# Four graph layers on one core: result scatters, shared queries, edge slots and weight parts moved in a hand-written order

## The chip, the cores and the metric

The kernel runs on one core of one Trainium2 chip. A core has five engines that run at the same time[...]: TensorE (PE, matmuls; its weight loads are listed as PEld), VectorE (DVE), ScalarE (ACT), GpSimd (POOL), and SyncE (SP), which here only issues DMAs. POOL issues DMAs too, those with indices (gathers and scatters). Each engine takes its instructions in the order in which the program lists them for it. The metric is the device time of one execution in microseconds. Before the change its median over three runs is 2139.91 us, from 2137.19 to 2143.26.

## The reference

A batch of 16 graphs shares one adjacency matrix of 1024 nodes in which an entry is set with probability 0.0078, so that a node has 8 neighbours on average. Node features have width 128. Layers 0, 2 and 3 are attention layers with 8 heads of 16 and a feed-forward part; layer 1 is a graph attention layer. Cut to what matters:

```python
def attention_layer(adj, h):                     # layers 0, 2, 3
    Q, K, V = h @ Wq, h @ Wk, h @ Wv             # per head: 8 heads of 16
    scores = where(adj == 0, -inf, Q @ K.T / 4)
    x = layer_norm(h + softmax(scores) @ V @ Wo + bo)
    return layer_norm(x + relu(x @ W1 + b1) @ W2 + b2)

def graph_layer(x, adj):                         # layer 1
    h = x @ W
    e = leaky_relu((h @ a_src)[:, None] + (h @ a_dst)[None, :], 0.2)
    return layer_norm(softmax(where(adj == 0, -inf, e)) @ h + x)

x = attention_layer(adj, x); x = graph_layer(x, adj)
x = attention_layer(adj, x); x = attention_layer(adj, x)
```

## The kernel before

The kernel uses the sparsity: it lists the neighbours of every node and touches only those (`sparse_path`). A second path for other matrices, `dense_path`, is skipped by a flag.

**Setup.** `graph` sorts the nodes by degree and finds, with VectorE's eight-largest instruction, the list of neighbours of each node. In the sorted order the nodes form 8 row blocks of 128. `slots` turns the lists of one block into gather indices (`idx`) and 0/1 matrices (`marks`): its inner function `spread` lays the lists out with small TensorE matmuls (L433, L441) into a PSUM bank; then VectorE reads that bank (L454 to L470). In the kernel before, the generator stops once after `spread`, then `WAIT` = 3 times more with the word "pass", then does the VectorE part. `load_weights` loads a layer's weights and prepares them: it centres Wo and W2 on VectorE (L485 to L487), multiplies W1 with b2 on TensorE (L524) and subtracts that from b1 on VectorE (L529). `load_graph_weights` does the like for layer 1: a transposition, a copy `wgT` (L551), a product with the two end vectors, a copy of it (L555), and a centring.

**Blocks.** The main loop runs over 64 units, here called blocks: 4 layers, 2 groups of 8 graphs, 8 row blocks. Blocks 0 to 7 are group 0 of layer 0, 8 to 15 its group 1, 16 to 31 layer 1, 32 to 47 layer 2, 48 to 63 layer 3. A block of an attention layer has five parts. A part handles two chunks; a chunk is one neighbour for each of 128 slots. The fourth part has a single chunk, the shared one, whose slots are taken from several neighbour columns. For every part:

- `gathered` issues on POOL one indirect DMA per chunk, the neighbours' keys and values (`e<-table,idx`, L968), four parts ahead, into one of four buffers; so it waits until VectorE has finished with the part that used the buffer.
- `products` multiplies keys and expanded queries on VectorE (L982). For the shared chunk POOL does this (L997, `product_of_shared`) two parts ahead, in place in the buffer `qx`, which SP filled before with pieces of the expanded queries (`shared`, DMA `qx<-qr`, L946). `qx` is single: it is free again when TensorE has summed the shared chunk of the block before.
- `exponentials` reduces the products on VectorE (L1015) and takes the exponential on ScalarE (L1019).
- `weighted`, one part later, multiplies values and exponentials on VectorE (L1043).
- `summed`, two parts later, adds the chunks with matmuls against `marks` into PSUM (L1059). When a block's last part is summed, `divided` sums the exponentials, takes reciprocals (L1096), divides (L1099) and starts two tails, one for each half of the group.

**Between the parts.** `others()` stands at three places of every part and hands out other work in small steps. From block 1's second part on a table (`PLANS`) tells which: "a" and "b" are a step of the tail of the first and second half; "q" is a step of `aside()`. A tail (`attention_tail`) does the output projection, the norms and the feed-forward part of the block before, on TensorE and ScalarE. Its end, `finish`, either transposes the new features and projects them for the next layer (stored on SP as `kept<-xT`, L575, and `table<-kv`, L592), or, in layer 3, transposes the result back, copies it on ScalarE (`outs`, L660) and issues on POOL the scatter of the result (L699, once per block; the very last block uses L693). `aside()` takes one step of the first generator in `fronts`; if that list is empty, of `loads` (the fetch of x for a block ahead, in layer 0 an indirect DMA and transpositions); and if both are empty, of `slow`, which in blocks 0 to 6 projects group 1 of layer 0 at leisure (`at_leisure`, L583 and L592). In the first two blocks one step of `slow` is handed out at every `others()` as well. What is left in `fronts` at the end of a block is done there at once.

**What stands in fronts.** For block 0: the five steps of the slots of block 1, the rest of the fetch of block 1 (`second`), the weight parts, the graph weight parts; in its second part the queries of block 1 are put behind all these. `queries` projects the queries on TensorE (L923), copies them (L927), repeats them over 128 partitions with matmuls (L932) and copies that (`qr`, L935). For each later block: in layer 0 the five steps of the slots of the next block, then the queries of the next block; in the fifth blocks of layers 1 and 2 (blocks 20 and 36) the weight parts of the next layer come before the queries.

In this order the instructions of all engines are written out; nothing is rearranged. Within a part, the order on POOL is: what `others()` brings (a scatter in layer 3), then `gathered`, then `product_of_shared`. `shared` comes in a block's second part, after `exponentials`:

```python
            others()
            if here:
                exponentials(i)
            if here and i == begun + 1:
                if is_attention(u):
                    shared(u)
```

Of the kernel before, what the change touches and what calls it, by code (L numbers as in the profile page):

```python
# [131 lines left out]
EDGES = 4  # L132
WAIT = 3
AHEAD = 4
# [11 lines left out]
def sparse_path(ctx: ExitStack, tc: tile.TileContext, a: dict, out: bass.AP, flag):  # L146
# [278 lines left out]
    def slots():  # L425
# [21 lines left out]
        for q in range(T):  # L447
            ps = spread(q)
            yield
            for _ in range(WAIT if q else 0):  # L450
                yield "pass"
            c, m = COLUMN[q, MIX, 0], MARK[q, 0, 0]
# [39 lines left out]
    def load_weights(layer):  # L492
# [35 lines left out]
        yield  # L528
        nc.vector.tensor_tensor(w[layer, "b1"], w[layer, "b1"], ps, ALU.subtract)  # L529
        nc.vector.tensor_tensor(w[layer, "ln1_b"], w[layer, "ln1_b"], w[layer, "b2"], ALU.add)  # L530
# [3 lines left out]
    def load_graph_weights():  # L534
# [15 lines left out]
        wgT = wts.tile([P, P], F32, tag="Wo", name="wgT")  # L550
        nc.vector.tensor_copy(wgT, ps)  # L551
        ps = bank([P, 2])
        nc.tensor.matmul(ps, wgT, ends, start=True, stop=True)
        yield
        nc.vector.tensor_copy(wg[:, D:], ps)  # L555
        centred(wg[:, :D], D)
# [109 lines left out]

    leaving = {}

    def finish(l, g, t, h, z, gain, shift, dve=False):
# [22 lines left out]
        if (l, g, t) == units[-1]:  # L692
            nc.gpsimd.indirect_dma_start(  # L693
                out=out.rearrange("n (k c) -> (n k) c", k=GR * HF),
                out_offset=bass.IndirectOffsetOnAxis(ap=halves[:, h : h + 1], axis=0),
                in_=o[:, h].rearrange("p g d -> p (g d)"), in_offset=None,
            )
        elif h + 1 == HF:
            nc.gpsimd.indirect_dma_start(  # L699
                out=out.rearrange("n (k c) -> (n k) c", k=GR),  # L700
                out_offset=bass.IndirectOffsetOnAxis(ap=places[:, g, t : t + 1], axis=0),
                in_=o.rearrange("p h g d -> p (h g d)"), in_offset=None,
            )

# [481 lines left out]
    with tc.manual_schedule():  # L1186
# [4 lines left out]
        next(entry)  # L1191
        more = [weights, load_graph_weights()]
        rest = slots()
# [31 lines left out]
        gathered(AHEAD - 1)  # L1225
        fronts.extend([islice(rest, WAIT + 2), second] + more)
        closing, sizes = None, ()
        begun = 0
        for i in range(len(parts) + 2):
            here = i < len(parts)  # L1230
            u = parts[i][0] if here else len(units)
            if here:
                l = units[u][0]
                eager[0] = 1 if u < 2 else 0
                if i and parts[i - 1][0] != u:
                    begun = i
                    if u < T - 1:
                        fronts.append(islice(rest, WAIT + 2))
                    if l + 1 < len(LAYERS) and LAYERS[l + 1][1] is ATTN:
                        if units[u][1:] == (0, 1):  # L1240
                            more = load_weights(LAYERS[l + 1][0])
                            next(more)
                            next(more)
                        if units[u][1:] == (0, 4):
                            fronts.append(more)
                if is_attention(u):
                    products(i)
            if i > 1:
                summed(i - 2)
                done = parts[i - 2][0]  # L1250
                if parts[i - 1 : i] == [] or parts[i - 1][0] != done:
                    closing = divided(done)
                    next(closing)
            others()
            if here:
                exponentials(i)
            if here and i == begun + 1:
                if is_attention(u):
                    shared(u)
                while loads:  # L1260
                    advance(loads)
                if u + 1 < len(units):
                    fronts.append(queries(u + 1))
                loads.append(loaded(u + 2))
# [3 lines left out]
            if 0 < i <= len(parts):  # L1268
# [4 lines left out]
                gathered(i - 1 + AHEAD)  # L1273
                product_of_shared(i + 2)
                for _ in sizes:
                    pass
# [27 lines left out]
        while opening[0] < len(plan[0]):  # L1304
            planned()
        while tails:
            advance(tails)
# [439 lines left out]
```

## Time and profile before

| what | value |
|---|---|
| median of 3 runs | 2139.91 us (2137.19 to 2143.26) |
| the profiled execution | 2128.25 us, span of its instructions 2126.4 us |
| first product of block 0 | 91.6 us |
| layer 0, blocks 0 to 7 and 8 to 15 | 306.4 and 269.5 us |
| layer 1 (16 blocks) | 316.5 us |
| layer 2 (16 blocks) | 536.7 us |
| layer 3 (16 blocks, with the end) | 605.7 us |
| mean granted TensorE clock | 0.973 |

The stretches in the table run from the first VectorE product of one block to that of another (L982; in layer 1 the first sum L1024). A line of a group of instructions in the profile reads: line of the kernel, engine, operation, output<-inputs with shapes, count, then busy time and mean duration in ns, then the idle time of the engine just before them and what ended it. A line of the chain of waits reads: who waited, for whom, us in total, times, the longest. Matmul counts are of the trace, in which each fp32 matmul can appear twice.

### The profile page before, as it was taken

The numbers are of one execution on the slowest core, as the hardware profiler recorded it, in microseconds if no ns is written. First come the engines' busy times: TensorE is split into PE (matmuls) and PEld (weight loads), VectorE is DVE, ScalarE is ACT, GpSimd is POOL, SyncE is SP. The second block draws the span as 40 slices with busy tenths as digits, with TensorE's granted clock in tenths as the row PEclk, the third lists the DMA queues.
The fourth block names the chain that finished last, engine by engine and source line by source line (L and its number), as shares of the span: only waits on it lengthen the run. The fifth ranks groups of instructions, "written<-read, shape, count | busy, mean of one in ns | idle before, by whom it ended". The sixth has DMA issues, their size and how long they took to land.

```text
span 2126.4 us, 37294 instructions
## 1 busy us (share of the span) xinstructions
PE 1955.3 (92%) x13444; PEld 1240.3 (58%) x13444; DVE 1818.9 (86%) x1320; ACT 1516.5 (71%) x5043; POOL 1173.0 (55%) x747
## 2 busy tenths in 40 slices
PE   7679999999999989998899999999999999999986
PEld 6455666656666555555465665666655555555544
DVE  6977889999997576677989999999998989988983
ACT  3447878888886555555587888888887787777764
POOL 3344555555556477684555555555555666656550
PEclk8789999999999999999999999999999999999998
DMA  7988888888998799998899999999998888788960
GB/s 271 347 283 287 316 295 297 305 298 305 316 314 297 234 338 355 320 365 310 311 321 323 329 339 314 331 336 337 332 314 274 301 277 306 249 298 279 296 223 22
DMA packets 164800, 636.10 MB, mean 299 GB/s; under 512 B 34664, under 2 KB 37480, under 8 KB 116110
## 3 DMA queue, kind: packets, MB, share of 16 engines
q0 software_dynamic: 88720, 485.08, 64.6%
q1 hardware_dynamic: 75888, 148.57, 21.6%
q8 instruction: 108, 1.77, 0.3%
q14 instruction: 84, 0.69, 0.1%
HBM read 581.08 MB, written 92.34 MB: 317 GB/s over the span
## 4 chain that ended last, share of the span: by engine, by line
PE 47%; DVE 17%; DMA 14%; issue 13%; POOL 5%; ACT 4%; POOLq 0%; DVEq 0%; ACTq 0%
DMA e<-table,idx 13%; PE acc L1059 12%; DVE pr L1043 5%; PE yps L752 5%; PE ps L738 5%; PE ps L654 5%; DVE pr L982 4%; POOL e L968 4%; PE ps L583 3%; PE ps L932 3%; DVE sc L1015 3%; PE yps L756 2%; PE yps L728 2%; PE yps L727 2%; PE ps L923 2%
## 5 line engine op out<-in xcount | busy, mean ns | idle before, releaser
L968 POOL DMA_INDIRECT e<-table,idx x576 | 890.2, 1545 | 683.9 <-DVE pr L1043 417.9
L1043 DVE TENSOR_TENSOR pr<-e,ex 128x2048 f32<-128x2048 f32 x272 | 630.0, 2325 | 76.7 <-ACT ex L1019 38.4
L1059 PE MATMUL acc<-pr,marks 128*32 128x512 f32 x2200 | 442.8, 621 | 57.5 <-DVE pr L1043 43.9
L982 DVE TENSOR_TENSOR pr<-e,qr 128x2048 f32<-128x2048 f32 x192 | 440.4, 2294 | 43.1 <-ACT qr L935 21.0
L1015 DVE TENSOR_REDUCE sc<-pr 128x128 f32<-128x2048 f32 x192 | 438.9, 2286 | 6.6
L631 ACT ACTIVATE z<-yps,root 128x128 f32<-128x128 f32 x888 | 314.3, 372 | 175.7 <-PE yps L756 124.6
L1059 PEld LDWEIGHTS acc<-pr,marks 128*32 128x32 f32 x2200 | 93.9, 111 | 292.6 <-issue 204.2
L752 PE MATMUL yps<-W,f 128*128 128x128 f32 x1520 | 249.8, 282 | 7.5 <-ACT f L747 5.6
L647 ACT ACTIVATE z<-yps,rstd 128x128 f32<-128x128 f32 x888 | 252.2, 369 | 3.5
L752 PEld LDWEIGHTS yps<-W,f 128*128 128x128 f32 x1520 | 203.5, 191 | 65.4 <-ACT f L747 29.0
L935 ACT COPY qr<-ps 128x512 f32<-128x512 f32 x384 | 204.0, 600 | 16.7 <-PE ps L932 15.8
L583 PE MATMUL ps<-Wkv,xT 128*128 128x256 f32 x768 | 199.7, 406 | 15.2 <-ACT xT L662 7.4
L587 ACT COPY kv<-ps 128x512 f32<-128x512 f32 x176 | 102.6, 587 | 140.2 <-PE ps L583 120.5
L738 PE MATMUL ps<-x,W 128*128 128x512 f32 x384 | 187.0, 610 | 1.3 <-issue 0.9
L631 ACT ACTIVATION_READ_ACCUMULATOR z<-yps,root 128x1 f32 x888 | 187.4, 211 | 0.0
L583 PEld LDWEIGHTS ps<-Wkv,xT 128*128 128x128 f32 x768 | 146.1, 200 | 59.7 <-issue 15.8
L654 PE MATMUL ps<-ident,z 128*128 128x128 f32 x896 | 151.9, 286 | 20.9 <-ACT z L647 11.3
L997 POOL TENSOR_TENSOR qx<-e,qx 128x1024 f32<-128x1024 f32 x48 | 134.4, 2800 | 62.3 <-DMA qx<-qr 34.5
L747 ACT ACTIVATE f<-ps,b 128x512 f32<-128x512 f32 x190 | 127.5, 692 | 49.2 <-PE ps L738 48.0
L727 PE MATMUL yps<-Wo,oT 128*128 128x128 f32 x768 | 155.4, 285 | 2.1 <-ACT oT L660 1.9
L728 PE MATMUL yps<-centre,x 128*128 128x128 f32 x768 | 154.4, 283 | 2.1 <-ACT x L723 0.2
L932 PE MATMUL ps<-q,rep 32*128 32x512 f32 x768 | 141.3, 640 | 8.5 <-ACT q L927 7.7
(178 smaller groups left out, 2794.9 us busy)
## 6 DMA issues: line engine op xcount, KB each, us to landing
table<-kv SPq DMA_DIRECT2D x88, 512.0 KB
kept<-xT SPq DMA_DIRECT2D x96, 256.0 KB
x<-kept SPq DMA_DIRECT2D x48, 512.0 KB
qx<-qr SPq DMA_DIRECT2D x54, 256.0 KB
e<-table,idx POOLq DMA_INDIRECT x576
table<-kv SPq DMA_DIRECT2D x32, 256.0 KB
qx<-qr SPq DMA_DIRECT2D x48, 128.0 KB
qx<-qr SPq DMA_DIRECT2D x12, 384.0 KB
```

The costliest lines, as they stand in the source:

```text
L583: nc.tensor.matmul(ps[:, k, :], x[:, i + k, :], w[LAYERS[l][0], "Wkv"], start=True, stop=True,)
L631: nc.scalar.activation(z[:, i, :], y[:, i, :], AF.Square, scale=D**-0.5, bias=root, accum_out=total[:, i : i + 1],)
L647: nc.scalar.activation(z[:, i, :], y[:, i, :], AF.Copy, scale=rstd[:, i : i + 1])
L654: nc.tensor.transpose(ps[:, i, :], z[:, i, :], ident)
L738: nc.tensor.matmul(ps, p["W1"][:, f * P : (f + 1) * P], x1.rearrange("p g n -> p (g n)"), start=True, stop=True,)
L752: nc.tensor.matmul(ps[:, i, :], f1[:, f, i * P : (i + 1) * P], p["W2"][:, f, :], start=(f == 0), stop=False,)
L932: nc.tensor.matmul(ps, rep_of(j), q[32 * j : 32 * j + 32], start=True, stop=True)
L968: nc.gpsimd.indirect_dma_start(out=es[i][:, k, :], out_offset=None, in_=tables[l, g][:, :], in_offset=bass.IndirectOffsetOnAxis(ap=idx[:, ...
L982: nc.vector.tensor_tensor(prs[i][0][:, :n, :], es[i][:, :n, :ROW], of_piece(qs[u], piece), ALU.mult,)
L1015: nc.vector.tensor_reduce(sc[:, :n, :], prs[i][0][:, :n, :].rearrange("p k (a d) -> p k a d", d=HD), mybir.AxisListType.X, ALU.add,)
L1043: nc.vector.tensor_tensor(prs[i][k0 // 2][:, :m, :].rearrange("p k (a d) -> p k a d", d=d), es[i][:, k0 : k0 + m, base : base + ROW].rearr ...
L1059: nc.tensor.matmul(outs[32 * j : 32 * j + 32], marks[:, mark, :], rhss, start=(chunk == mine[0]), stop=(chunk == mine[-1]),)
```

## The change

Five edits, all of order or of engine:

- **Scatters.** In layer 3 `finish` puts the scatter of a block on a list, `ready`. The main loop issues what is on the list after `gathered` and `product_of_shared`, and once more at the end.
- **Shared queries.** `shared` is called in a block's first part, before its first `others()`, not in its second part.
- **Slots.** The stops with "pass" are gone. The slots of block 1 are begun before the main loop and finished in block 0's second part; those of block 2 are made in block 1's first and second part; from then on those of block u + 2 are begun in the fourth part of block u and finished, on VectorE, in its fifth part after `exponentials`.
- **Order of fronts.** The queries of the next block are put at the head; in block 0 they are put ahead of the weight parts. The graph weight parts are handed out in block 1 and have three empty steps before the centring.
- **Weight parts.** The subtraction from b1 becomes two ScalarE activations, and the copies `wgT` and of the end columns go to ScalarE.

```diff
@@ slots
-            for _ in range(WAIT if q else 0):
-                yield "pass"
@@ load_weights
-        nc.vector.tensor_tensor(w[layer, "b1"], w[layer, "b1"], ps, ALU.subtract)
+        for f in range(F):
+            one = w[layer, "b1"][:, f : f + 1]
+            nc.scalar.activation(one, ps[:, f : f + 1], AF.Identity, bias=one, scale=-1.0)
@@ load_graph_weights
-        nc.vector.tensor_copy(wgT, ps)
+        nc.scalar.copy(wgT, ps)
...
-        nc.vector.tensor_copy(wg[:, D:], ps)
+        nc.scalar.copy(wg[:, D:], ps)
+        for _ in range(3):
+            yield
         centred(wg[:, :D], D)
@@ finish
+    ready = []
...
-            nc.gpsimd.indirect_dma_start(
+            rows = o.rearrange("p h g d -> p (h g d)")
+            ready.append(lambda: nc.gpsimd.indirect_dma_start(
                 out=out.rearrange("n (k c) -> (n k) c", k=GR),
                 out_offset=bass.IndirectOffsetOnAxis(ap=places[:, g, t : t + 1], axis=0),
-                in_=o.rearrange("p h g d -> p (h g d)"), in_offset=None,
-            )
+                in_=rows, in_offset=None,
+            ))
@@ before the main loop
-        more = [weights, load_graph_weights()]
+        ends = load_graph_weights()
+        more = [weights, ends]
...
-        fronts.extend([islice(rest, WAIT + 2), second] + more)
+        next(rest)
+        fronts.extend([second, weights])
...
+        slot = ()
@@ main loop, a block's first part
-                    if u < T - 1:
-                        fronts.append(islice(rest, WAIT + 2))
+                    if u == 1:
+                        fronts.append(ends)
@@ main loop
+            if here and i == begun and is_attention(u):
+                shared(u)
+            if here and (i == 5 or i == begun + 3 and 0 < u < T - 2):
+                slot = islice(rest, 1)
+                fronts.insert(0, slot)
             others()
             if here:
                 exponentials(i)
+                if i in (1, 6) or i == begun + 4 and 0 < u < T - 2:
+                    for _ in slot:
+                        pass
+                    for _ in islice(rest, 1):
+                        pass
             if here and i == begun + 1:
-                if is_attention(u):
-                    shared(u)
                 while loads:
                     advance(loads)
                 if u + 1 < len(units):
-                    fronts.append(queries(u + 1))
+                    fronts.insert(0 if u else len(fronts) - 1, queries(u + 1))
...
                 gathered(i - 1 + AHEAD)
                 product_of_shared(i + 2)
+                while ready:
+                    ready.pop(0)()
...
         while opening[0] < len(plan[0]):
             planned()
+        while ready:
+            ready.pop(0)()
```

More of the change, by code (lines that the diff above doesn't have):

```diff
@@ L132 @@
 EDGES = 4
-WAIT = 3
 AHEAD = 4
```

## The prediction

> **What bounds the kernel now.** I read the page first: no engine is free enough to be ignored, and none is full.
>
> ```profile
> span 2126.4 us, 37294 instructions
> PE 1955.3 (92%) x13444; PEld 1240.3 (58%) x13444; DVE 1818.9 (86%) x1320; ACT 1516.5 (71%) x5043; POOL 1173.0 (55%) x747
> ```
>
> A mean over stages says little, so I cut the span at the first product (L982, in layer 1 L1024) of a block and asked for busy time by stretch. In order: blocks 0 and 1 of layer 0; blocks 2 to 7; blocks 8 to 15 (its second group); blocks 37 to 47 (layer 2, settled); blocks 49 to 62 (layer 3). Columns: stretch, length, then busy us of PE, weight load, DVE, ACT, POOL.
>
> ```profile
> 91.60:173.20 81.60, 64.72 (x406) 42.31 (x407) 64.78 (x57) 38.60 (x95) 35.26 (x22) 0.83 0.83 298
> 173.20:398.00 224.80, 213.50 (x1658) 140.27 (x1657) 194.35 (x137) 179.08 (x607) 120.65 (x72) 1.00 0.86 299
> 398.00:667.50 269.50, 256.79 (x1817) 165.21 (x1816) 253.67 (x137) 218.79 (x773) 153.30 (x95) 0.99 0.88 307
> 1158.00:1520.60 362.60, 359.73 (x2433) 231.85 (x2432) 345.38 (x187) 300.25 (x968) 201.97 (x121) 1.00 0.96 332
> 1553.40:2040.70 487.30, 453.74 (x3001) 278.45 (x2999) 447.82 (x240) 370.16 (x1207) 289.67 (x168) 0.98 0.85 286
> ```
>
> Layer 2 settled is TensorE's: idle 2.9 of 362.6 us, 33.0 us a block. Layer 3 has fewer matmuls a block (3001/14 = 214 against 2433/11 = 221), yet takes 487.3/14 = 34.8 us, with TensorE idle 33.6 us and VectorE idle 39.5. Blocks 0 and 1 leave both idle 17 us. Blocks 2 to 15 are nearly TensorE's: idle 11.3 and 12.7 us.
>
> Next, the groups by shape of those two settled stretches (the first two lines layer 2, the other four layer 3; mean ns of one after the busy time, then idle before).
>
> ```profile
> L1043 DVE TENSOR_TENSOR pr<-e,ex 128x2048 f32<-128x2048 f32 x44 | 104.8, 2381 | 6.3 <-ACT ex L1019 4.1 <-ACT z L647 1.7 <-issue 0.4
> L1059 PE MATMUL acc<-pr,marks 128*32 128x512 f32 x352 | 70.0, 598 | 0.1
> L1043 DVE TENSOR_TENSOR pr<-e,ex 128x2048 f32<-128x2048 f32 x56 | 141.9, 2533 | 1.3 <-ACT ex L1019 1.3
> L1059 PE MATMUL acc<-pr,marks 128*32 128x512 f32 x448 | 105.1, 639 | 25.1 <-DVE pr L1043 25.1
> L1015 DVE TENSOR_REDUCE sc<-qx 128x64 f32<-128x1024 f32 x14 | 17.0, 1212 | 18.8 <-POOL qx L997 18.8
> L699 POOL DMA_INDIRECT out<-outs,places x13 | 16.8, 1290 | 84.1 <-ACT both L1109 76.1 <-ACT outs L660 8.0
> ```
>
> In layer 3 POOL sits 84.1 us in front of the scatter of results (L699), which waits for ScalarE's copy of the results. VectorE's weighting is 152 ns longer on average, its reduction of the shared product waits 18.8 us for POOL, and TensorE waits 25.1 us for the weighting; in layer 2 these are 0.1 us or nothing. The timeline of block 51 shows the link (POOL lines, then VectorE):
>
> ```profile
> 1638.93 1.02 POOL L699 DMA_INDIRECT out<-outs,places  x1 [4.36 <-ACT outs L660]
> 1640.26 2.91 POOL L968 DMA_INDIRECT e<-table,idx  x1 [0.30 <-DMA e<-table,idx]
> 1644.49 2.36 POOL L997 TENSOR_TENSOR qx<-e,qx 128x1024 f32<-128x1024 f32 x1
> 1642.32 2.29 DVE L1015 TENSOR_REDUCE sc<-pr 128x128 f32<-128x2048 f32 x1
> 1644.52 4.48 DVE L1043 TENSOR_TENSOR pr<-e,ex 128x2048 f32<-128x2048 f32 x1
> ```
>
> The scatter stands ahead of two gathers and POOL's product L997. The product therefore starts when VectorE begins a weighting, which takes 4.48 instead of 2.28 us.
>
> Last, the chain of waits for the other edits: each line is waiter, releaser, total us, times, longest.
>
> ```profile
> POOL qx L997 <- DMA qx<-qr: 34.5, 13, 4.6
> DVE pr L982 <- ACT qr L935: 21.0, 8, 9.9
> DVE little L454 <- PE ps L441: 10.6, 4, 2.7
> DVE b L529 <- PE ps L524: 7.8, 2, 6.7
> ...
> 132.83 2.29 DVE L982 TENSOR_TENSOR pr<-e,qr 128x2048 f32<-128x2048 f32 x1 [8.33 <-ACT qr L935]
> ```
>
> The last line, from VectorE's timeline, is block 1's first product: 8.33 us late for its expanded queries.
>
> [...] L1043 at 4.48 us beside L997, while L1015 keeps 2.29. [...] in block 50 POOL stood 9.85 us before the scatter, with gathers behind it whose buffer had been read by 1599.98.
>
> **The change part by part.**
>
> *Scatter (L699) behind the gathers and the product, layer 3.* No instruction is added; 15 scatters move past two gathers and L997. In block 51 VectorE's release of the gather buffer was at 1638.22, so gathers can start near 1638.5 instead of 1640.26, and the product 1.8 us earlier, mostly under the reduction. In block 50 they can start at 1600.2 instead of 1608.20. What VectorE loses now: 56 x (2533 - 2280) ns = 14.2 us, plus 18.8 = 33.0 us, 2.36 a block. The residue I expect is layer 2's, 44 x (2381 - 2280) ns = 4.4 us in 11 blocks, 0.40 each. So VectorE regains 14 x 1.96 = 27 us. TensorE can regain its 25.1 us of waits, and no more unless its own work is packed closer. The lower of the two, less a little for blocks where TensorE was behind anyway (VectorE waited 7.1 us for denominators): 22. Block 63 has one more such wait of 3.3 us, behind which TensorE stood 2.5: another 2. Taken: **-24**; bounds -32 (both regained, plus the 7.9 us that L982 waits for gathers) and -8 (TensorE sets the pace at once). The scatter's own wait then comes after the product, before the next gathers; in block 50 the results are copied at 1605.89 and VectorE frees the next gather buffer at 1611.52. That cover of 5.6 us hides it; without it, the wait would again cost up to 9.85 us.
>
> *Blocks 0 and 1.* Block 1's queries (8 projecting and 8 expanding matmuls, 10 copies) go ahead of the weight parts, the graph weights leave for block 1, three empty turns of the slot generator vanish, and the fetch of block 2's x starts in block 0. What goes: VectorE's 8.33 us; on TensorE 2.0 us before block 1's projection of queries, 2.6 at 138.4 (a knock-on: ScalarE's copy stands behind an exponential that waits for the late product) and 2.9 at 147.6 (transposes waiting for x). TensorE's 7.5 is the smaller, and its 3.8 us wait for block 1's x stays since that fetch is not moved. Taken: **-7**; bounds -12 and +3 (an extra half of leisure work, near 2.2 us of TensorE, falls into block 0).
>
> *Slots ahead, and expanded queries (`shared`) a part earlier, blocks 2 to 15.* Slots: same instructions (about 1.4 us of VectorE a block), the 10.6 us wait gone since a whole part lies between matmul and use. `shared`: 2 to 4 DMAs a block move on SP ahead of the stores of the next layer's x, which held them: in block 12 the last sum over the old ones ended 9.25 us into the block, and the new ones went out at 13.35. L997 starts up to 4 us earlier; in blocks 8 to 15 [...] 32 x (2451 - 2280) ns = 5.5, plus 4.5 = 10 us of VectorE. But TensorE's idle is 24 us over 14 blocks, 1.7 each, and layer 2's settled residue is 0.26 each, so at most 20; most of it is scattered in waits below 1 us that no edit touches. Taken: **-6**; bounds -14 and +10 (stores delayed, below). In layers 2 and 3 SP already waits for TensorE's last sum over the old queries, so the move is nothing there.
>
> *Weight parts on ScalarE.* Per layer one VectorE subtraction (156 ns) becomes two activations; the nearest row, a 128x2 copy from PSUM, is 200 ns: +0.4 us of ScalarE, three times. wgT and the two end columns add about 0.6 us once. The wait moves too: in block 20 VectorE stood 6.7 us for L524 and TensorE then 2.5 for VectorE; in block 36, 1.2 and 1.5. Now ScalarE waits, with the next exponential and the tails' norms behind it. VectorE has two weightings of 2.3 us to do meanwhile, so most is covered. Taken: **-3**; bounds -4 and +3.
>
> Sum: -24 - 7 - 6 - 3 = -40. The profiled execution took 2128.25 us (span 2126.4, so 1.9 around it); the sum puts it at 2088. The median of the runs shown is 2139.91, 11.7 above that execution; less 40 it is **2100 us**.
>
> **The rivals.** *TensorE takes the pace in layer 3 and layer 0 gives nothing*: matmul queues are busy 453.7 of 487.3 us there, and gaps close only in part. Then -20: 2120. For it: 93% busy. Against it: the gaps are single waits on VectorE, and layer 2 does more matmuls in less time. *Closer packing*: TensorE's busy time in layer 3 holds stretched sums (639 against 598 ns), so both engines regain all upper bounds of the first two parts: -55, 2085. *Slower: the SP queue.* The earlier expanded-query DMAs wait for TensorE's last sum, 8 to 14 us into a layer 0 block, with stores of x and tables behind them. ScalarE's projection copies have two buffers; it stood 7.0 us for such stores in blocks 0 and 1. A hold of 40/14 = 2.9 us in each of blocks 2 to 15 cancels everything; 4 us gives 56 - 40 = +16, 2156. Against it: stores in block 3 left at 10.33 and 11.01, the sum ended at 11.81, so they are delayed 2 to 4 us at a time when the copies need them 6 us later. *No net change*: [...] product against L982 instead of L1043, 2140.
>
> **How the numbers follow.** Likeliest case 0.58 (2100, own range 2088 to 2112); TensorE's pace 0.20 (2112 to 2130); closer packing 0.08; no net change 0.07; slower 0.07. Runs of this kernel spread 2137 to 2143, so a difference below 0.3% (6.4 us) cannot be told from none. The range 2086 to 2126 leaves out the two last cases, half of closer packing and a fringe: about 2 in 10. Faster 0.86, same 0.07, slower 0.07.
>
> **What would show it.** Right: POOL's idle before L699 after the product; L1043 in layer 3 near 2.38 us, L1015's wait for POOL near nothing, blocks 49 to 62 near 33.2 us; block 1's first product without its 8 us; L454 and L529 gone from VectorE's waits; POOL's wait for expanded queries below 10 us. Wrong: layer 3's blocks stay near 34.8 us with TensorE busy throughout, or ScalarE's copies wait for table stores in layer 0, or exponentials wait behind the biases in block 20.

## The result, and the profile after

The changed kernel took 2127.84 us (median of 20 runs, 2119.39 to 2133.71), the kernel before 2139.76 us on the same chip (20 runs, 2128.08 to 2147.18). The ratio, with its 95% interval, is 0.9947 [0.9934, 0.996]: 12 us faster, or 0.5%. The forecast was 2100 us, so 28 of the 40 us did not come, and the time lies 1.8 us above the range. In short: the largest term of the forecast, the moved scatter, brought nothing, and the 12 us come from the other edits.

The profiled execution of before (2128.25 us) was a short one of its kind; a second one, profiled later, took 2137.12, and that of after 2126.89. Profiles are therefore compared stretch by stretch, and whole times by medians.

The first view of after is the page's top: the span, and the busy time of the engines.

```profile
span 2125.0 us, 37303 instructions
PE 1972.9 (93%) x13444; PEld 1244.8 (59%) x13444; DVE 1806.1 (85%) x1315; ACT 1519.5 (72%) x5051; POOL 1182.4 (56%) x747
```

TensorE is busy 17.6 us longer than before with the same 13444 matmul records; VectorE is busy 12.8 us less. Next the same five stretches as in the prediction: blocks 0 and 1, 2 to 7, 8 to 15, 37 to 47 (layer 2), 49 to 62 (layer 3). Columns: stretch, length, busy us of PE, weight load, DVE, ACT, POOL, then granted clock, DMA share, GB/s.

```profile
91.30:179.50 88.20, 69.58 (x478) 45.36 (x479) 63.95 (x62) 42.81 (x106) 35.17 (x22) 0.85 0.85 304
179.50:397.10 217.60, 207.48 (x1584) 134.39 (x1583) 195.28 (x131) 174.92 (x599) 118.60 (x73) 1.00 0.86 300
397.10:666.40 269.30, 256.77 (x1811) 164.50 (x1810) 250.97 (x137) 218.82 (x773) 155.46 (x95) 0.99 0.87 305
1154.00:1518.40 364.40, 360.08 (x2431) 231.79 (x2430) 347.82 (x187) 300.64 (x967) 200.74 (x121) 1.00 0.95 329
1551.90:2039.00 487.10, 469.59 (x3023) 284.93 (x3022) 433.54 (x239) 371.60 (x1213) 295.67 (x169) 0.99 0.82 285
```

Layer 3, which was to give 24 us, takes 487.1 us as against 487.3: nothing. Blocks 0 and 1, which were to give 7, are 6.6 us longer, and blocks 2 to 7 are 7.2 us shorter.

Why nothing in layer 3? Here are the groups of that stretch by shape; they answer to lines of before that the prediction shows or that stand below (the kernel's lines moved by three: L982 is now L985, L1015 L1018, L1043 L1046, L1059 L1062, L997 L1000, L699 L702).

```profile
L985 DVE TENSOR_TENSOR pr<-e,qr 128x2048 f32<-128x2048 f32 x57 | 130.5, 2290 | 45.7 <-DMA e<-table,idx 33.9 <-PE ps L741 11.8
L1046 DVE TENSOR_TENSOR pr<-e,ex 128x2048 f32<-128x2048 f32 x56 | 128.8, 2301 | 1.6 <-ACT ex L1022 1.4
L1062 PE MATMUL acc<-pr,marks 128*32 128x512 f32 x448 | 102.1, 599 | 7.1 <-DVE pr L1046 6.7
L702 POOL DMA_INDIRECT out<-outs,places x13 | 39.5, 3037 | 2.0 <-issue 1.4 <-ACT x L726 0.3
L1018 DVE TENSOR_REDUCE sc<-qx 128x64 f32<-128x1024 f32 x14 | 16.9, 1211 | 0.0
```

All that the step promised is there. The weighting L1046 takes 2301 ns where it took 2533; the reduction L1018 waits for POOL not at all (18.8 us before); TensorE waits 7.1 us in front of its sums (25.1 before); POOL stands 2.0 us before the scatter (84.1 before). And all of it is spent again in the first line: VectorE's products of keys and queries wait 45.7 us, where they waited 8.5, for the neighbours' keys and values. In before their line read:

```profile
L982 DVE TENSOR_TENSOR pr<-e,qr 128x2048 f32<-128x2048 f32 x57 | 130.7, 2293 | 8.5 <-DMA e<-table,idx 7.9 <-issue 0.4
```

The waits of the whole execution say the same: first before, then three lines of after.

```profile
DVE pr L982 <- DMA e<-table,idx: 16.0, 24, 1.5
```
```profile
DVE pr L985 <- DMA e<-table,idx: 45.1, 24, 4.1
...
DVE pr L985 <- ACT qr L938: 14.2, 7, 9.4
...
DVE little L451 <- PE ps L440: 11.7, 5, 3.8
```

The trace points to the scatter's own line: issuing one scatter now takes POOL 3037 ns, not 1290. The timeline of block 51, POOL, shows where it stands (start, length, and idle time before it in brackets):

```profile
1637.09 3.71 POOL L1000 TENSOR_TENSOR qx<-e,qx 128x1024 f32<-128x1024 f32 x1
1640.95 3.06 POOL L702 DMA_INDIRECT out<-outs,places  x1
1644.32 2.98 POOL L971 DMA_INDIRECT e<-table,idx  x1 [0.31 <-ACT z L648]
1647.61 1.88 POOL L971 DMA_INDIRECT e<-table,idx  x1 [0.30 <-issue]
```

and VectorE's beside it:

```profile
1640.81 2.28 DVE L1046 TENSOR_TENSOR pr<-e,ex 128x2048 f32<-128x2048 f32 x1
1643.01 1.21 DVE L1018 TENSOR_REDUCE sc<-qx 128x64 f32<-128x1024 f32 x1
1644.13 2.28 DVE L1046 TENSOR_TENSOR pr<-e,ex 128x2048 f32<-128x2048 f32 x1
...
1656.53 2.29 DVE L985 TENSOR_TENSOR pr<-e,qr 128x2048 f32<-128x2048 f32 x1 [4.46 <-PE ps L741]
```

The scatter starts 0.14 us after the start of a weighting and ends 0.92 us after its end. The gather buffer is free at 1643.1, but the scatter holds POOL until 1644.0. When the gather starts at 1644.3, the next weighting has just begun (1644.13), and this gather takes 2.98 us, the next one 1.88. The two gathers are out at 1649.5, 6.4 us after the buffer came free. They are for the next block's first part, whose product then starts 4.46 us late (the profile names a matmul as releaser here, in nine of the twelve blocks the gather; the DMA engines' mean share is 1.00 until half a microsecond before this product starts). At the end of each of blocks 51 to 62 this wait is 3.1 to 4.5 us; in before it was 0 to 1.5.

Two short stretches of the same block, in the columns of the stretches above, show what that does to the transfers:

```profile
1642.50:1647.50 5.00, 4.78 (x36) 2.74 (x36) 5.00 (x4) 4.07 (x15) 4.50 (x2) 1.00 0.31 123
1648.00:1656.00 8.00, 7.88 (x44) 4.70 (x38) 4.04 (x3) 5.99 (x22) 6.44 (x6) 1.00 1.00 335
```

For 5 us the DMA engines are 31% busy; then their share is 1.00 over 8 us (335 GB/s, after 123), and the first product waits for what they bring. That it is the late issue, and not the scatter's own bytes in the way, a finer view shows: the busy tenths of the DMA engines from 1640 us on, half a microsecond to a digit (9 is 90% or more).

```profile
DMA  6999321008970000968998999899458979999999
```

The scatter was out at 1644.0, and the short burst from 1644.5 on moved 0.52 MB, which is the scatter's 128 x 1024 f32. Then the engines stand idle from 1646 to 1648, while POOL is still issuing the first gather (out at 1647.3).

### The profile page after: what moved, and what is told of

It is laid out like the page before. It is cut to its first block, busy times and chain, and to the rows that moved or that the text cites. A ratio compares the mean times of both kernels' runs of the same rounds, so it can differ in the third digit from the quotient of the medians.

```text
span 2125.0 us, 37303 instructions
## 1 busy us (share of the span) xinstructions
PE 1972.9 (93%) x13444; PEld 1244.8 (59%) x13444; DVE 1806.1 (85%) x1315; ACT 1519.5 (72%) x5051; POOL 1182.4 (56%) x747
## 4 chain that ended last, share of the span: by engine, by line
PE 49%; DVE 15%; DMA 11%; issue 9%; ACT 6%; POOL 2%; POOLq 0%; DVEq 0%; SPq 0%; ACTq 0%
PE acc L1062 13%; DMA e<-table,idx 10%; PE ps L655 5%; PE yps L755 5%; PE ps L741 5%; DVE pr L985 5%; DVE pr L1046 5%; PE ps L584 4%; DVE sc L1018 4%; PE ps L935 3%; PE yps L730 2%; PE yps L731 2%; PE yps L759 2%; PE ps L926 2%; POOL e L971 2%
## 5 line engine op out<-in xcount | busy, mean ns | idle before, releaser
L971 POOL DMA_INDIRECT e<-table,idx x576 | 877.4, 1523 | 763.2 <-DVE pr L1046 512.4
L1046 DVE TENSOR_TENSOR pr<-e,ex 128x2048 f32<-128x2048 f32 x272 | 617.7, 2280 | 76.9 <-ACT ex L1022 38.8
L985 DVE TENSOR_TENSOR pr<-e,qr 128x2048 f32<-128x2048 f32 x192 | 442.9, 2307 | 75.5 <-DMA e<-table,idx 45.1
L1062 PE MATMUL acc<-pr,marks 128*32 128x512 f32 x2200 | 437.2, 608 | 33.1 <-DVE pr L1046 19.9
L1018 DVE TENSOR_REDUCE sc<-pr 128x128 f32<-128x2048 f32 x192 | 438.9, 2286 | 6.6
L1062 PEld LDWEIGHTS acc<-pr,marks 128*32 128x32 f32 x2200 | 94.3, 110 | 266.6 <-issue 200.5
L655 PE MATMUL ps<-ident,z 128*128 128x128 f32 x896 | 159.3, 290 | 23.2 <-ACT z L648 13.7
L1000 POOL TENSOR_TENSOR qx<-e,qx 128x1024 f32<-128x1024 f32 x48 | 148.4, 3092 | 57.8 <-DMA e<-table,idx 17.5
L935 PE MATMUL ps<-q,rep 32*128 32x512 f32 x768 | 151.6, 646 | 9.4 <-ACT q L930 7.4
L655 PEld LDWEIGHTS ps<-ident,z 128*128 128x128 f32 x896 | 109.0, 143 | 79.6 <-ACT z L648 29.2
```

What stands on the lines that cost most here:

```text
L655: nc.tensor.transpose(ps[:, i, :], z[:, i, :], ident)
L935: nc.tensor.matmul(ps, rep_of(j), q[32 * j : 32 * j + 32], start=True, stop=True)
L971: nc.gpsimd.indirect_dma_start(out=es[i][:, k, :], out_offset=None, in_=tables[l, g][:, :], in_offset=bass.IndirectOffsetOnAxis(ap=idx[:, ...
L985: nc.vector.tensor_tensor(prs[i][0][:, :n, :], es[i][:, :n, :ROW], of_piece(qs[u], piece), ALU.mult,)
L1018: nc.vector.tensor_reduce(sc[:, :n, :], prs[i][0][:, :n, :].rearrange("p k (a d) -> p k a d", d=HD), mybir.AxisListType.X, ALU.add,)
L1046: nc.vector.tensor_tensor(prs[i][k0 // 2][:, :m, :].rearrange("p k (a d) -> p k a d", d=d), es[i][:, k0 : k0 + m, base : base + ROW].rearr ...
```

## The experiments

A ratio is to the kernel before on the same chip, with a 95% interval. Kernels measured together share one chip. The median of before was 2136.02 us beside the scatter alone, the scatter put back, the scatter in the idle place and before once more; 2133.95 beside the scatter behind the first gathers, the weight parts, the shared queries and the order alone; 2134.70 beside the last three.

**The scatter alone, put into the kernel before.**

```diff
-            nc.gpsimd.indirect_dma_start(...)          # finish, layer 3
+            ready.append(lambda: nc.gpsimd.indirect_dma_start(...))
...
                 gathered(i - 1 + AHEAD)
                 product_of_shared(i + 2)
+                while ready:
+                    ready.pop(0)()
```

> The kernel before with the scatter edit alone (result scatters issued behind the gathers and the shared product). Theory 'moved wait': in layer 3 the scatter takes about 3 us to issue under a VectorE weighting and stands ahead of the next block's first gathers, so that a new wait of 3 to 4 us for those gathers[...]: blocks 49 to 62 stay at 34.8 us each (+-0.4), L1015's wait for POOL is gone, and the time is within 5 us of before. Rival 'it is the scatter that gives the whole measured gain': blocks 49 to 62 shorter by 0.8 us each, the time 10 to 14 us below before.

Measured: 2134.69 us, ratio 0.9997 [0.9981, 1.0013]; blocks 49 to 62 take 492.3 us. Its groups in that stretch, by shape:

```profile
L984 DVE TENSOR_TENSOR pr<-e,qr 128x2048 f32<-128x2048 f32 x56 | 133.0, 2374 | 40.3 <-DMA e<-table,idx 36.6 <-PE ps L740 3.7
L1045 DVE TENSOR_TENSOR pr<-e,ex 128x2048 f32<-128x2048 f32 x56 | 130.3, 2327 | 1.4 <-ACT ex L1021 1.4
L701 POOL DMA_INDIRECT out<-outs,places x13 | 39.2, 3017 | 2.1 <-issue 1.6 <-ACT q L929 0.2 <-ACT x L725 0.2
```

The trade is the same as in after: short weightings, a scatter of 3 us, 40.3 us of waits for gathers. The largest term of the forecast is worth nothing by itself (-0.6 us, from -4 to +3).

**The changed kernel with the scatter put back.** The reverse of that diff.

> The changed kernel with the scatter edit undone. Theory 'moved wait': the scatter edit is worth nothing, so this one is as fast as the changed kernel, 2128 us (+-4), with layer 3 as in the kernel before (L1015's wait for POOL near 18 us). Rival 'the scatter gives the gain': 2136 to 2142 us.

Measured: 2123.19 us, 0.9927 [0.9902, 0.9951]; blocks 49 to 62 take 486.1 us. The interval overlaps that of the change (0.9934 to 0.996), so here too the scatter's move gives nothing; the time is 0.8 us below the 2124 to 2132 expected. All of the 12 us comes from the other edits.

**The changed kernel with the scatter in POOL's idle place.** If the move failed because of what stands behind the scatter, a place with nothing urgent behind it should give the gain. POOL has one in a block's first part, around the gather for the fourth part, where it waits for a buffer. The scatter goes out there, a block later than in the kernel before; so the expectations below call this kernel "the scatter a block later".

```diff
+                if i == begun:
+                    while ready:
+                        ready.pop(0)()
                 gathered(i - 1 + AHEAD)
                 product_of_shared(i + 2)
-                while ready:
-                    ready.pop(0)()
```

> The changed kernel with the scatters issued at another place: in the next block's first part, ahead of the gather of its fourth part, where POOL sits 3.9 us waiting for VectorE in the traces. Theory 'moved wait': with neither the product nor the next block's first gathers behind the scatter, both waits are gone and blocks 49 to 62 fall to the 33.0 to 33.6 us of layer 2: 15 to 25 us below the changed kernel, 2103 to 2113 us. Rival 'layer 3 is held by its transfers or by TensorE': 34.5 us a block wherever the scatter stands, 2124 to 2132 us.

Measured: 2098.95 us (2092.51 to 2103.56), 0.9814 [0.9789, 0.984]: faster than both kernels, and 4 us faster than the expected 2103 to 2113. Blocks 49 to 62 take 462.1 us, 33.0 each. The groups:

```profile
L1046 DVE TENSOR_TENSOR pr<-e,ex 128x2048 f32<-128x2048 f32 x56 | 137.0, 2446 | 0.7 <-ACT ex L1022 0.7
L985 DVE TENSOR_TENSOR pr<-e,qr 128x2048 f32<-128x2048 f32 x57 | 130.5, 2289 | 4.3 <-DMA e<-table,idx 3.8 <-issue 0.3
...
L702 POOL DMA_INDIRECT out<-outs,places x12 | 35.4, 2950 | 3.7 <-issue 3.7
...
L1018 DVE TENSOR_REDUCE sc<-qx 128x64 f32<-128x1024 f32 x14 | 16.9, 1210 | 6.8 <-POOL qx L1000 6.8
```

The scatter's issue still lasts 2950 ns, nearly as long as in after, so the length alone does no harm. The wait for gathers falls from 45.7 to 4.3 us. Part of VectorE's loss to POOL is back (weightings of 2446 ns, 2301 in after, and 6.8 us of waiting for POOL), and yet this is the faster kernel. Its timeline of block 51, POOL:

```profile
1622.86 2.95 POOL L702 DMA_INDIRECT out<-outs,places  x1 [0.30 <-issue]
1626.12 1.90 POOL L971 DMA_INDIRECT e<-table,idx  x1 [0.30 <-issue]
1631.91 0.99 POOL L971 DMA_INDIRECT e<-table,idx  x1 [3.90 <-DVE pr L1046]
...
1637.10 2.35 POOL L1000 TENSOR_TENSOR qx<-e,qx 128x1024 f32<-128x1024 f32 x1 [2.90 <-DMA e<-table,idx]
1641.87 1.03 POOL L971 DMA_INDIRECT e<-table,idx  x1 [2.42 <-DVE pr L1046]
1643.20 2.60 POOL L971 DMA_INDIRECT e<-table,idx  x1 [0.30 <-ACT z L648]
```

POOL stands idle 3.90 us soon after the scatter, which is what absorbs it. Later, with the product done at 1639.45 and nothing in the way, the first gather leaves 0.3 us after its buffer is free (weighting over at 1641.60), under a reduction of VectorE, in 1.03 us; both are out 4.2 us after the release instead of 6.4.

**The scatter behind the next block's first gathers.** A place between the two: those gathers go first, but the scatter is still ahead of the product and of later gathers.

```diff
                 gathered(i - 1 + AHEAD)
+                if i > begun + 1:
+                    while ready:
+                        ready.pop(0)()
                 product_of_shared(i + 2)
-                while ready:
-                    ready.pop(0)()
```

> The changed kernel with the scatter issued one part later, behind the next block's first gathers. Theory 'moved wait': what costs is only what stands behind the scatter on POOL. Now the first gathers are free of it and the second part's gathers stand behind it, with VectorE still busy on this block for a part longer, so part of the wait is covered: blocks 49 to 62 at 33.2 to 34.2 us each, the time 2106 to 2120 us, between the changed kernel and the one with the scatter a block later. Rival 'only POOL's idle place helps, since the scatter's bytes hold up the gathers in the transfer engines': 34.8 us a block, 2124 to 2132 us.

Measured: 2107.44 us, 0.9875 [0.9843, 0.9906]; blocks 49 to 62 take 472.9 us. The group that matters:

```profile
L985 DVE TENSOR_TENSOR pr<-e,qr 128x2048 f32<-128x2048 f32 x57 | 132.2, 2320 | 26.2 <-DMA e<-table,idx 24.7 <-issue 1.1
```

The wait for gathers is 26.2 us, between 4.3 and 45.7, and the time too lies between. It has moved to the gathers that now stand behind the scatter: 19.6 us of it are in front of the later products of a block, where after has none. The scatter's issue is also shorter here (1912 ns on average). Over the three places the time follows the wait for gathers: what counts is which gathers stand behind the scatter.

These kernels, the second profile of before and one kernel from below stand here in one ledger of VectorE, blocks 49 to 62, in us. "Collisions" is the weighting's busy time above 56 x 2.28 us plus the reduction's wait for POOL; "gathers" is the idle time in front of the products (L982) and their busy time above 2.28 us each. 2.28 us is the median of the 124 weightings of this shape that ran in before while POOL was idle; the 4 such products took 2.28 to 2.29.

| kernel | collisions | gathers | sum | length | length less sum |
|---|---|---|---|---|---|
| before | 14.2 + 18.8 | 8.5 + 0.7 | 42.2 | 487.3 | 445.1 |
| before, second profile | 11.3 + 25.3 | 4.4 + 0.5 | 41.5 | 485.8 | 444.3 |
| scatter alone | 2.6 + 0 | 40.3 + 5.3 | 48.2 | 492.3 | 444.1 |
| after, scatter put back | 10.9 + 22.1 | 9.2 + 0.7 | 42.9 | 486.1 | 443.2 |
| after | 1.1 + 0 | 45.7 + 0.5 | 47.3 | 487.1 | 439.8 |
| scatter behind first gathers | 3.9 + 0 | 26.2 + 2.2 | 32.3 | 472.9 | 440.6 |
| scatter in the idle place | 9.3 + 6.8 | 4.3 + 0.5 | 20.9 | 462.1 | 441.2 |
| the same, order undone | 6.6 + 2.3 | 6.6 + 1.6 | 17.1 | 460.3 | 443.2 |

The last column stays within 439.8 to 445.1. So VectorE's own account carries layer 3 to within some 5 us in all eight, and the five other profiled kernels fall inside the same bounds (440.5 to 444.0). A straight line fitted to all thirteen gives 1.03 us of length per us of collisions and 0.99 per us of gathers (an estimate): a microsecond of waiting for gathers costs as much as one of collision.

**The kernel before once more.**

> The kernel before once more, for a second profile: the two traces differ by 1.4 us in their spans, the medians by 12. Theory 'a short execution was traced': the span is now near the median, 2134 to 2142 us, and the stretch in which it is longer than the first trace tells where the measured gain lies. Rival 'a traced execution always runs some 10 us shorter': 2124 to 2129 us again.

Measured: 2137.12 us, span 2135.2. Against the first profile: blocks 0 and 1 85.1 us (81.6), blocks 8 to 15 275.5 (269.5), layer 1 312.8 (316.5), the end 90.4 (85.7), blocks 49 to 62 485.8 (487.3). A stretch can thus differ by 6 us between two executions of one kernel, and only differences well above this are read from stretches below.

**The weight parts on ScalarE, in the kernel before.**

```diff
-        nc.vector.tensor_tensor(w[layer, "b1"], w[layer, "b1"], ps, ALU.subtract)
+        for f in range(F):
+            one = w[layer, "b1"][:, f : f + 1]
+            nc.scalar.activation(one, ps[:, f : f + 1], AF.Identity, bias=one, scale=-1.0)
...
-        nc.vector.tensor_copy(wgT, ps)
+        nc.scalar.copy(wgT, ps)
...
-        nc.vector.tensor_copy(wg[:, D:], ps)
+        nc.scalar.copy(wg[:, D:], ps)
```

> The kernel before with the weight parts on ScalarE alone (b1, wgT, end columns), no order changed. Theory 'the gain is block 20 and 36': block 20 falls from 19.4 to about 16.5 us and block 36 by about 1 us, the rest as before: 3 to 5 us below the kernel before, 2131 to 2134 us. Rival 'the gain is in the order of layer 0': within 2 us of before.

Measured: 2126.66 us, 0.9967 [0.995, 0.9983], that is -7 us (-4 to -11). Block 20 shows it plainly. Of the kernel before, VectorE's waits there:

```profile
DVE b L529 <- PE ps L524: 6.7, 1, 6.7
```

and of this one, ScalarE's:

```profile
ACT b L531 <- PE ps L524: 1.9, 1, 1.9
```

VectorE's wait of 6.7 us becomes one of 1.9 us on ScalarE, and the block takes 16.55 us, where it took 19.4 in all six profiled kernels without this edit. Block 36 takes 33.9 us (34.2 to 35.5 without). These two make some 4 of the 7 us. Expected were 3 to 5; what the rest is stays open.

**The shared queries early, in the kernel before.**

```diff
+            if here and i == begun and is_attention(u):
+                shared(u)
             others()
...
-                if is_attention(u):
-                    shared(u)
```

> The kernel before with the shared queries' transfers a part earlier, nothing else. POOL's wait for them falls from 34 us to below 10. Theory 'TensorE holds layer 0': blocks 8 to 15 stay at 269 to 276 us and the time is within 4 us of before. Rival '[...]': blocks 2 to 15 some 8 to 14 us shorter, 2122 to 2129 us.

Measured: 2133.61 us, 0.9991 [0.9976, 1.0005]: no difference. Its waits of POOL and of VectorE, and VectorE's of before:

```profile
POOL qx L997 <- DMA qx<-qr: 1.6, 2, 1.2
```
```profile
DVE sc L1015 <- POOL qx L997: 32.0, 10, 3.3
```
```profile
DVE sc L1015 <- POOL qx L997: 31.1, 11, 3.3
```

POOL's wait for the pieces of the queries is gone (34.5 us in before). VectorE's wait for POOL looks unchanged, but that total mixes two layers. In layer 0, blocks 0 to 15, it was 9.0 us in before (8.9 in its second profile) and is gone here. The rest is nearly all layer 3: 22.1 and 28.6 us in the two profiles of before, 29.8 here. So the edit does free VectorE of 9 us in layer 0, and the time does not show it (-2 us, from -5 to +1). This fits the first theory, that TensorE holds layer 0, but a gain of a few us is not ruled out.

**The order alone, in the kernel before**: slots a block ahead, the queries at the head of `fronts`, the graph weights in block 1, `shared` left in its old place.

```diff
-        fronts.extend([islice(rest, WAIT + 2), second] + more)
+        next(rest)
+        fronts.extend([second, weights])
...
+            if here and (i == 5 or i == begun + 3 and 0 < u < T - 2):
+                slot = islice(rest, 1)
+                fronts.insert(0, slot)
...
-                    fronts.append(queries(u + 1))
+                    fronts.insert(0 if u else len(fronts) - 1, queries(u + 1))
```

> The kernel before with the slots and the order of fronts changed (slots a block ahead, queries ahead of the weights, graph weights in block 1), without the scatters, the shared queries and ScalarE's weight parts. Theory 'leisure work moves from block 6 to block 1': block 1 about 10 us longer, block 6 about 6 us shorter, blocks 0 to 7 together within 3 us of before, so the time within 4 us of before. Rival 'this edit gives the measured gain': 8 to 12 us below before, 2124 to 2128 us, with blocks 0 to 7 that much shorter.

Measured: 2136.78 us, 1.0006 [0.9987, 1.0025]: no difference. Its waits of POOL and VectorE show a new fault:

```profile
POOL qx L996 <- DMA qx<-qr: 52.2, 11, 12.9
```
```profile
DVE sc L1014 <- POOL qx L996: 62.4, 19, 10.8
```

With the order changed but `shared` late, VectorE waits 62.4 us for the shared product, as against 31.1. In layer 0 alone it waits 30.4 us, as against 9.0. (The profile is of the longest of its 14 executions, 2144.46 us.)

**The order and the shared queries together.** Both diffs above.

> The kernel before with the order of fronts and slots and the earlier shared queries, without the scatters and ScalarE's weight parts. The order alone let POOL wait 52 us for the shared queries (34 before). Theory 'the two belong together': with the earlier transfers that wait falls to about 10 us and the pair gives 3 to 6 us, which with the 7 us of the weight parts makes up the measured 12: 2128 to 2132 us. Rival 'both are worth nothing': within 2 us of before, so that the measured gain is the weight parts and chance.

Measured: 2127.23 us, 0.9959 [0.9944, 0.9974], that is -9 us (-5.5 to -12). VectorE's wait for POOL is back at 29.7 us, none of it in layer 0. Neither edit shows a gain alone, and together they give 9 us. It fits this that early queries repair what the order spoils (30.4 us of VectorE's waits in layer 0), so that a gain of the order shows; it is not shown what that gain consists of. Where the 9 us lie the single profiles don't tell (spans of one kernel differ by as much). A hint: blocks 8 to 15 take 269.0 to 272.0 us in the eight profiled kernels with early shared queries, and 269.5 to 280.7 in the five profiles without.

**The fastest kernel with the order undone**: weight parts, early shared queries and the scatter in the idle place, on the kernel before.

```diff
-        next(rest)
-        fronts.extend([second, weights])
+        fronts.extend([islice(rest, WAIT + 2), second] + more)
...
-                    fronts.insert(0 if u else len(fronts) - 1, queries(u + 1))
+                    fronts.append(queries(u + 1))
```

> The kernel with the scatter a block later, with the order of fronts and slots undone (so: weight parts on ScalarE, shared queries early, scatter a block later). Theory 'order is worth little where leisure work only moves': within 4 us of the kernel with the order, 2097 to 2105 us. Rival 'the order gives what the sum of the single edits lacks': 2105 to 2110 us.

Measured: 2100.86 us, 0.9845 [0.9823, 0.9868], against 0.9814 [0.9789, 0.984] with the order. The intervals overlap. With the pair above (0.9959 against 0.9991) it is the second comparison in which the order is worth about 0.3%, and in both this is at the edge of what the runs can tell. Blocks 0 and 1 take 82.6 us here and 91.1 with the order; blocks 2 to 7 take 224.8 and 217.4.

**The fastest kernel with leisure work eager in block 0 only.**

```diff
-                eager[0] = 1 if u < 2 else 0
+                eager[0] = 1 if u < 1 else 0
```

> The kernel with the scatter a block later, and leisure work handed out at every call in block 0 alone instead of blocks 0 and 1. Theory 'work moved into block 1 is dear': in blocks 0 and 1 TensorE's granted clock is 0.83 to 0.85 against 1.00 from block 2 on; block 1 falls by 8 to 12 us and blocks 2 to 7 grow by 4 to 10, net 0 to 6 us faster than the kernel with the scatter a block later, 2093 to 2099 us. Rival 'work only moves': within 2 us.

Measured: 2102.61 us, 0.9846 [0.9823, 0.9869]: not faster. Blocks 0 and 1 take 79.9 us instead of 91.1, blocks 2 to 7 229.8 instead of 217.4. The 11.2 us saved come back as 12.4. But 3.1 of the 11.2 are block 0, whose work is the same in both kernels, and the profile is of the longest of five executions (2110.13 us); the expected 2093 to 2099 us did not come.

## Why the prediction was right and wrong

Term by term, in us (intervals in brackets; the order and the shared queries were not separable, as the experiments show):

| part of the change | forecast | measured |
|---|---|---|
| scatter | -24 | -0.6 [-4, +3], alone |
| blocks 0 and 1; slots and shared queries | -7 - 6 = -13 | -9 [-12, -5.5], together |
| weight parts | -3 | -7 [-11, -4], alone |
| all | -40 | -12 |

**The direction was right, and the sum of the three smaller terms by luck.** With the scatter put back, the other edits measure 0.9927 x 2136.02 - 2136.02 = -15.6 us (-10 to -21; the medians differ by 12.8); the forecast had -7 - 6 - 3 = -16. One by one they were mis-sized, and the errors cancel: the weight parts give 4 us more than forecast (the interval touches the bound of -4), the order with the shared queries 4 us less.

**The scatter term failed: -24 forecast, nothing measured.** The step that failed is the end of its paragraph: the scatter's wait "then comes after the product, before the next gathers", and "That cover of 5.6 us hides it". Only the wait for the data was weighed there, and that wait is indeed hidden (POOL's idle before the scatter is 2.0 us). The scatter's issue, and the gathers that stand behind it, were put at nothing. The line shown of block 51 had the issue at 1.02 us, and I did not ask what VectorE does at the new place. There it lasts 3.04 us, and the queue behind it begins with the next block's first gathers. Both are stretched in turn (2.98 and 1.88 us in block 51) and out 6.4 us after the release of their buffer, where the kernel with the scatter in the idle place needs 4.2. The next block's first product waits 3.1 to 4.5 us. What stands behind the moved instruction was worked out for the old place and not for the new one. What VectorE regained (33.0 less 1.1 = 31.9 us of collisions) it lost to gathers (46.2 less 9.2 = 37.0); the rest of its account was 5.3 us shorter, so that the length stayed.

The term's size was right once the place was: moved to the idle place, the scatter gives 2123.19 - 2098.95 = 24 us against the kernel with it put back (the two share a chip). But not by the working given. Collisions fall by 16.9 us there (33.0 to 16.1), and 5 more come from gathers (9.9 to 4.8); the residue "of layer 2" (0.40 us a block) was too low: 16.1 us in 14 blocks is 1.15 each. That the two errors nearly cancel is luck.

**The rivals.** TensorE's pace was not it, although the time lies in its range (2112 to 2130) and its sign came: 34.8 us a block with TensorE busy 469.6 of 487.1 us. Nearly the same matmuls are busy 453.7 us in before and 443.4 in the kernel with the scatter in the idle place, which takes 462.1. So "93% busy" was no evidence for a bound. "No net change" had the right outcome for this term and the wrong cause: no collision came back (L985 takes 2290 ns, L982 in before 2293); a queue did. The SP queue's rival did not come: blocks 8 to 15 take 269.3 us (269.5 in before). Closer packing did not come either; its parts add up to -53 (32 + 12, and 6 + 3 as taken), not -55.

**Blocks 0 and 1: -7 forecast, 3 to 7 us longer measured.** The wait of block 1's first product for its queries did fall, from 8.3 to 1.3 us, as the step said. But one more half of leisure work falls into block 1, not block 0, and I had put it at 2.2 us of TensorE, as a bound. The slots of one more block, 40 matmul records, go the same way. Block 1 grows from 40.4 to 50.9 us, with TensorE busy 43.4 us instead of 32.6, while block 6, from which this work went, falls from 38.7 to 32.2. The granted clock is not the reason: in blocks 0 and 1 it is 0.85, and was 0.83. TensorE's wait for block 1's x, which I said stays at 3.8 us, grew to 7.9; the likely reason, not tested, is that the slots no longer stand ahead of it and the fetch itself was not moved. Twelve profiles bear the exchange out. Six have the new order with the same leisure work: blocks 0 and 1 take 87.7 to 91.1 us, blocks 2 to 7 215.7 to 219.6. Six have the old order: 79.3 to 85.1 and 223.3 to 225.2. Blocks 0 to 7 together take 305.1 to 308.5 and 304.5 to 308.4: the work moved, and nothing was gained.

**Shared queries early: right on the waits, unproven in worth.** POOL's wait fell below 10 us (9.6), and VectorE's wait for POOL in layer 0 from 9.0 us to 2.2. But alone the edit shows no gain in the time. What the runs show is that the new order needs it.

**Slots and weights.** L529 is gone from VectorE's waits. The wait of L454, now L451, is not: 11.7 us (10.6 in before), of which 7.1 in blocks 0 and 1. No exponential stood behind the biases: the new wait is 1.9 us.

## What to carry to other kernels

When an instruction is moved, work out the queue at the new place as at the old one: how long it lasts beside what runs there, what stands behind it, and who waits for that first. An issue of 1 us that becomes 3 in front of a prefetch can give back a 24 us gain, and the same 3 us (2.95 here) are free where the engine would stand idle anyway (3.90 us). A large wait in front of an instruction is a reason to move it, not a measure of what moving it brings. And a wait is read by stage: a total that stays at 31 us can hide 9 us that vanished in one layer.

## What the runs showed of the hardware

**The length of an indirect DMA's issue on POOL depends on what VectorE does.** In before, of 205 gathers that started while VectorE ran a product or weighting of the neighbours' keys and values (L982 and L1043), 202 lasted over 1.5 us (median of all 205: 2.61; longest 3.09). Of 175 that started under a reduction of such products none lasted over 1.03 us; of 44 under the division (L1099) none over 1.01; with VectorE idle, 87 lasted 0.98 to 1.01. After shows the same (200 of 203; none of 130 under reductions). A stretched one ends 0.86 to 0.89 us after VectorE's instruction does (202 in before, 200 in after). All 14 scatters that started under a weighting in after took 2.91 to 3.07 us. What in these instructions of VectorE stretches the issue is not shown: no run varied it alone.

**A product on POOL and one on VectorE lengthen each other; reductions kept their length.** In block 51 of after, POOL's product L1000 starts under a product of VectorE and takes 3.71 us. In before, as L997, it started 0.03 us ahead of a weighting and took 2.36, and that weighting took 4.48 instead of 2.28. Over the whole of before, 21 of POOL's products started under a product or weighting of VectorE and took 2.37 to 4.34 us (median 3.23); the 6 that met neither took 2.36 to 2.39. Of 29 reductions (L1015) that ran beside POOL's product in before none took over 2.29 us. (The one of block 51 that the prediction names did not run beside it for more than 0.12 us.)

**TensorE's recorded busy time is elastic.** The work of blocks 49 to 62 is busy 453.7 us (3001 records), 469.6 (3023) and 443.4 (2993) in before, in after and with the scatter in the idle place. The records differ by 1%, the busy time by 6%. The granted clock was 0.98, 0.99 and 1.00: it differs by 2% between the first and the third, as the busy time does (2.3%), but the second busy time is the longest at a clock between the two. The durations of the single records add up to 1139.5 us in after and 1124.3 with the scatter in the idle place: they overlap, so the time that they cover can change without their work changing.
